# Softmax denominators in a cross-attention kernel: computed in four column quarters ahead of the weighted sums, with a half-width reciprocal copied to all rows

## The chip, the cores and the metric

The kernel runs on one core of one Trainium2 chip. The core has a matrix engine (PE, whose weight loads are listed apart as PEld), a vector engine (DVE), an activation engine (ACT), a general engine (POOL) and a queue engine (SP) that issues transfers. Each engine works through its own instructions in the order in which they were issued, and waits on semaphores for the others. Matrix products land in PSUM; everything else lies in SBUF. The metric is the device time of one execution in microseconds (us); lower is better.

## The reference

The layer is cross-attention followed by a feed-forward network, in float32, on 2048 query rows of width 256 and 1601 context rows of width 192, with 16 heads of width 64 and one learned null key and value ahead of the context. What matters here, per head:

```python
x = layer_norm(x, g_norm)
q = x @ Wq
kv = context @ Wkv
k, v = jnp.split(kv, 2, axis=-1)
...
sim = jnp.einsum('bhid,bhjd->bhij', q, k)
sim = jnp.where(full_mask[:, None, None, :], sim, max_neg)
attn = jax.nn.softmax(sim.astype(jnp.float32), axis=-1)
out = jnp.einsum('bhij,bhjd->bhid', attn, v)
out = out.transpose(0, 2, 1, 3).reshape(b, -1, INNER)
out = out @ Wout
```

The softmax is a sum of exponentials over 1602 keys for each head and query, and the output of each head is divided by that sum. After it come a layer norm, a residual, three dense layers with weights of plus and minus one and rectifiers between them, and another residual.

## The kernel before

**Units.** The attention goes over units `(p, b)`: a pair `p` of heads (8 of them) and a block `b` of 512 queries (4 of them), 32 units, numbered 0 to 31 in this document as `u` is in the code. The keys lie on the partitions in 13 tiles of 128 (the last has 66). The order of the instructions is the order of the program text (`tc.manual_schedule()`), on every engine.

**One unit.** For each key tile `k`, `exps` multiplies keys and queries on PE (L393, both heads side by side in the two halves of the array's rows, into the PSUM tile `sT`), and ACT takes the exponential (L406) into an SBUF tile `e`. Between them PE forms the maxima of the next unit: `max_chunk` (L356) writes a PSUM tile of the pool `flex`, and DVE reduces it (L359). The pool `flex` has two buffers, so a new tile there waits until the tile before the last one has been read. POOL adds the 13 tiles `e` up into `acc` (L621 the first, L623 the others); it finishes them well into the next unit. Then `weighted` multiplies the values with the tiles `e` into the PSUM tile `av` (L413): 13 key tiles, two heads each, the heads in the two halves of the array's columns. A float32 matmul goes through the array in two passes, so it has two records in the trace.

**The denominators.** `acc` of the unit before (`last`) holds partial sums on 128 partitions. `divided` (L428 to L435) completes them: two matmuls with a matrix of ones, one for each head (L431), write the sum of each of the 512 queries to 64 rows each, so that the PSUM tile `den` has every sum in all the 64 rows of its head. DVE takes the reciprocal of all 128 by 512 numbers (L433) and multiplies the unnormalised output `avs` of that unit with it (L434), in the SBUF tile `aoT`. It is called at L650, behind the third of the 13 key tiles of `weighted`.

**Behind it.** ACT copies `av` into `avs` (L671; one buffer, so it waits until L434 of this unit has read the old one). PE turns the maxima (L369), multiplies `aoT` with the output weights (`project_out`, L421), and projects queries, keys and values for the units to come (L213, L238, L243, L298, L310). DVE adds the result to `y_sb` (L424 in the first head pair, L426 later).

**Units that do more.** In units 0 and 1 the input rows of units 2 and 3 are normalised: DVE statistics, then on ACT a square root, eight instructions in `centred_beside` (L143, L144) and a table load for the exponential (L644). Units 30 and 31 normalise finished rows in the same way (L635 is the table load of unit 30). All of this is issued ahead of `weighted`. In unit 31 there is no next unit, so no maxima; POOL first multiplies and adds the finished rows of block 0 (L599, L600), then sums the exponentials. In units 28 and 29 DVE also turns the first feed-forward weights into numbers (L655, L657).

**The feed-forward.** The denominators of unit 31 come behind the first group of the second dense layer (L779, tile `den_last`); behind them DVE normalises rows of block 1, POOL adds their residual (L122, L123), DVE normalises again (L89), and PE turns the result (L130) behind the third group. In the feed-forward each dense group is 16 or 32 matmuls at L720, and `halved` (L708 on ACT, L709 on DVE) splits its result in two parts.

Of the kernel before, what the change touches and what calls it, by code (L numbers as in the profile page):

```python
# [9 lines left out]
F32 = mybir.dt.float32  # L10
# [12 lines left out]
HEADS, DH = 16, 64  # L23
# [13 lines left out]
def xattn_ffn(ctx, tc, x, ctxT, mask, g_norm, null_kv, wq, wkv, wout, g_out, k0, k1, k2, s0, s1, s2, out):  # L37
    nc = tc.nc
# [8 lines left out]
    def flex(name):  # L47
        return ps_f.tile([128, 2, 512], F32, tag="f", name=name)

    def spare(name):  # L50
        return ps_s.tile([128, 2, 512], F32, tag="s", name=name)
# [14 lines left out]
    lp = ctx.enter_context(tc.tile_pool(name="later", bufs=2))  # L66
    ones = cp.tile([128, DH], F32, name="ones")
# [27 lines left out]
    def slot(name):  # L95
        nonlocal n_slots
        n_slots += 1
        return (flex, spare)[n_slots % 2](name)

    def norm_begin(b, src, name):  # L100

        mv = stats(src[:, ts(b, 4), :], 4, f"{name}{b}")
        r = sp.tile([128, 4], F32, tag="rstd", name=f"rstd_{name}{b}")
        norms[b] = (mv, r)

    def norm_root(b):
        mv, r = norms[b]
        nc.scalar.activation(r, mv[:, :, 1], AF.Sqrt, bias=eps_sb)

    def norm_end(b, dst, src, beside=False):  # L110
        mv, r = norms[b]
        nc.vector.reciprocal(r, r)
        if beside:
            centred_beside(dst, src, mv, r, b)
            return
        for j in range(4 * b, 4 * b + 4):
            centred(dst[:, j, :], src[:, j, :], mv, r, j - 4 * b)

    def residual(b, engine):

        for j in range(4 * b, 4 * b + 4):
            engine.tensor_tensor(y_sb[:, j, :], y_sb[:, j, :], gout_sb, ALU.mult)  # L122
            engine.tensor_tensor(x_sb[:, j, :], x_sb[:, j, :], y_sb[:, j, :], ALU.add)  # L123

    def turned(b):

        pt = slot(f"uT_{b}")
        for j in range(4):
            for c in range(2):
                nc.tensor.transpose(pt[:, c, ts(j, 128)], y_sb[:, 4 * b + j, ts(c, 128)], ident)  # L130
        hi = lp.tile([128, 2, 512], F32R, tag="uhi", name=f"uhi_{b}", bufs=1)
        lo = lp.tile([128, 2, 512], F32R, tag="ulo", name=f"ulo_{b}", bufs=1)
        nc.scalar.copy(hi, pt)
        nc.vector.tensor_tensor(lo, pt, hi.bitcast(F32), ALU.subtract)
        return hi, lo
# [10 lines left out]
    with ExitStack() as att:  # L146
# [262 lines left out]
        def weighted(p, k, e, av):  # L409
            v = pairs[p][1]  # L410
            n = rows_of(k)
            for j in range(2):
                nc.tensor.matmul(  # L413
                    av[ts(j, DH), 0, :], v[:n, k, ts(j, DH)], e[:n, j, :], start=k == 0, stop=k == KC - 1
                )

        def project_out(p, b, aoT):
            po = spare(f"po_{p}_{b}")
            pv = po.rearrange("p a (c d) -> p (a c) d", d=D)
            for t in range(4):  # L420
                nc.tensor.matmul(pv[:, t, :], aoT[:, ts(t, 128)], weights[p][3], start=True, stop=True)  # L421
            y = y_sb[:, ts(b, 4), :]
            if p == 0:
                nc.vector.tensor_copy(y, pv)  # L424
            else:
                nc.vector.tensor_tensor(y, pv, y, ALU.add)  # L426

        def divided(p, b, avs, acc, ps):  # L428

            for j in range(2):  # L430
                nc.tensor.matmul(ps[ts(j, DH), :], ones, acc[:, j, :], start=True, stop=True)  # L431
            aoT = lp.tile([128, 512], F32, tag="aoT", name=f"aoT_{p}_{b}", bufs=1)
            nc.vector.reciprocal(aoT, ps)  # L433
            nc.vector.tensor_tensor(aoT, avs, aoT, ALU.mult)  # L434
            return aoT  # L435

# [142 lines left out]
        last = None  # L579
        with tc.manual_schedule():  # L580
            for u, (p, b) in enumerate(units):
# [21 lines left out]
                acc = lp.tile([128, 2, 512], F32, tag="acc", name=f"acc_{p}_{b}")  # L603
# [40 lines left out]
                    nc.scalar.activation(warm, eps_sb, AF.Exp)  # L644

                av = spare(f"av_{p}_{b}")
                for k in range(KC):
                    weighted(p, k, es[k], av)
                    if k == 2 and last is not None:
                        aoT = divided(*last, flex(f"den_{p}_{b}")[:, 0, :])  # L650
                if u in (len(units) - 4, len(units) - 3):

                    half = k0_u8[:, 2 * (len(units) - 3 - u) :, :][:, 0:2, :]
# [16 lines left out]
                avs = lp.tile([128, 512], F32, tag="avs", name=f"avs_{p}_{b}", bufs=1)  # L670
# [17 lines left out]
                last = (p, b, avs, acc)  # L688
# [11 lines left out]
    def second_weights(engine, c):  # L700
        if engine is nc.scalar:
            nc.scalar.activation(w1[c], k1_u8[:, c, :], AF.Identity, bias=s1b[:, 1:2], scale=s1b[:, 0:1])
        else:
            engine.tensor_scalar(w1[c], k1_u8[:, c, :], s1b[:, 0:1], s1b[:, 1:2], ALU.mult, ALU.add)
# [6 lines left out]
    def layer_open(b, n):  # L711
        return [fp.tile([128, 8, 512], F32R, tag=f"h{n}{part}", name=f"h{n}{part}_{b}") for part in ("hi", "lo")]

    def layer_pair(b, n, g, out, w, parts, chunks):

        ps = slot(f"ps{n}_{b}_{g}")
        steps = [(c, part) for c in range(chunks) for part in range(2)]
        for i, (c, part) in enumerate(steps):
            for f in range(2):
                nc.tensor.matmul(  # L720
                    ps[:, f, :],
                    w(c)[:, ts(2 * g + f, 128)],
                    parts[part][:, c, :],
                    start=i == 0,
                    stop=i == len(steps) - 1,
                )
        halved(out[0][:, ds(2 * g, 2), :], out[1][:, ds(2 * g, 2), :], ps)

    def first(b, uT):
        h0 = layer_open(b, 0)  # L730
        for g in range(4):
            layer_pair(b, 0, g, h0, lambda c: w0[:, c, :], uT, 2)
            if b == 0 and g < 2:
                second_weights(nc.scalar, 2 + g)
        return h0
# [31 lines left out]
    with tc.manual_schedule():  # L767
        for c in range(2):
            second_weights(nc.scalar, c)
        for c in range(4, 8):  # L770
            second_weights(nc.gpsimd, c)
        nc.gpsimd.tensor_scalar(w2, k2_u8, 2.0, -1.0, ALU.mult, ALU.add)
        h0 = first(0, uT)
        for b in range(NB):
            h1 = layer_open(b, 1)
            for g in range(4):
                layer_pair(b, 1, g, h1, lambda c: w1[c], h0, 8)
                if b == 0 and g == 0:
                    aoT = divided(*last, slot("den_last")[:, 0, :])  # L779
                if b == 0 and g == 1:  # L780
                    project_out(*last[:2], aoT)
                if b + 1 < NB:
                    if g == 0:
                        norm_begin(b + 1, y_sb, "y")
                        norm_root(b + 1)
                        norm_end(b + 1, y_sb, y_sb)
                        residual(b + 1, nc.gpsimd)
                    if g == 1:
                        norm_begin(b + 1, x_sb, "r")
                        norm_root(b + 1)  # L790
                        norm_end(b + 1, y_sb, x_sb)
                    if g == 2:
                        uT = turned(b + 1)
            if b + 1 < NB:
                h0 = first(b + 1, uT)
            third(b, h1)
# [39 lines left out]
```

## Time and profile before

| | |
|---|---|
| time, median of 3 runs (lowest, highest) | 1310.03 us (1309.79, 1311.21) |
| the profiled execution | 1309.9 us, of which span 1308.1 us |
| PE busy | 1290.2 us (99%) |
| POOL busy | 997.9 us (76%) |
| DVE busy | 819.7 us (63%) |
| ACT busy | 624.7 us (48%) |
| denominators on PE (L431), share of the chain | 2% |
| reciprocal on DVE (L433), 31 of them | 104.0 us, 3356 ns each |
| mean granted TensorE clock | 0.996 |

The span is the time from the first instruction to the last; the execution has 1.8 us around it. The page of the profile lists busy time by engine, a chain of waits followed back from the last instruction, and groups of instructions by line. Groups have the busy time of the group, the mean duration of one, and the idle time of the engine before them with what ended it. A busy PE is not one at its peak, since matmuls are pipelined and their ends are modelled. Paces are read from starts here, not from durations of matmuls.

### The profile page before, as it was taken

To read this page: it belongs to the slowest core of one execution; us is meant where nothing else is said; L and a number is where in the kernel's file an instruction comes from. 1 tells how busy PE (TensorE), PEld (TensorE's weight loads), DVE (VectorE), ACT (ScalarE), POOL (GpSimd) and SP (SyncE) were. 2 spreads that over 40 slices of the span, in tenths; PEclk is the share of its full clock that TensorE was granted. 3 is DMA by queue.
4 is the path that set the end of the run, shared out by engine and by line. 5 is a ranking of instruction groups with operands and counts; after the bars stand their busy time and mean duration, and the time that the engine had idled before them with its cause. 6 is when DMAs were issued, how large, how long until landed. Compare 5 with 4: busy or idle time off the path is not lost.

```text
span 1308.1 us, 15963 instructions
## 1 busy us (share of the span) xinstructions
PE 1290.2 (99%) x6568; PEld 657.8 (50%) x6568; DVE 819.7 (63%) x822; ACT 624.7 (48%) x740; POOL 997.9 (76%) x503
## 2 busy tenths in 40 slices
PE   8989999999999999999999999999999999999998
PEld 6334444444444444444444444444444443688887
DVE  7877666666666666666666666666666784554431
ACT  4576444444444444454555555555555457321121
POOL 4768988898889888998889888988898999611100
PEclk9989999999999999999999999999999999999999
DMA  6100000000000000000000000000000010000000
GB/s 143 21 1 5 1 1 13 6 1 1 13 5 1 1 13 5 1 1 5 9 5 1 1 13 5 1 1 5 1 17 1 1 41 1 1 9 9 17 17 17
DMA packets 16122, 13.18 MB, mean 10 GB/s; under 512 B 2656, under 2 KB 15520, under 8 KB 16048
## 3 DMA queue, kind: packets, MB, share of 16 engines
q1 hardware_dynamic: 14928, 11.02, 3.2%
q8 instruction: 52, 0.85, 0.3%
q10 hardware_dynamic: 640, 0.79, 0.2%
q0 software_dynamic: 480, 0.34, 0.2%
q14 instruction: 22, 0.18, 0.0%
HBM read 10.04 MB, written 2.10 MB: 9 GB/s over the span
## 4 chain that ended last, share of the span: by engine, by line
PE 91%; DVE 3%; ACT 2%; POOL 2%; DMA 1%; issue 1%; SPq 0%; DVEq 0%; POOLq 0%; ACTq 0%
PE sT L393 28%; PE av L413 26%; PE ps L720 9%; PE max L356 7%; PE psq L213 4%; PE po L421 4%; PE ps L746 2%; PE den L431 2%; PE psv L298 2%; PE psk L238 2%; PE sT L404 1%; DVE mx L359 1%; POOL acc L623 1%; PE psv L310 1%; DMA x_sb<-in_x 1%; PE psk L243 1%
## 5 line engine op out<-in xcount | busy, mean ns | idle before, releaser
L623 POOL TENSOR_TENSOR acc<-acc,e 128x1024 f32<-128x1024 f32 (+1 forms) x352 | 847.0, 2406 | 27.6
L359 DVE TENSOR_REDUCE mx<-max 128x2 f32<-128x1024 f32 x384 | 452.0, 1221 | 81.4 <-PE max L356 81.3
L406 ACT ACTIVATE e<-sT,maskb 128x1024 f32<-128x1024 f32 (+1 forms) x416 | 459.6, 1113 | 42.0 <-PE sT L404 11.8
L393 PE MATMUL sT<-qT,kT 64*128 64x512 f32 (+1 forms) x1664 | 448.5, 612 | 0.8 <-ACT e L406 0.2
L413 PE MATMUL av<-e,v 128*64 128x512 f32 (+1 forms) x1664 | 369.5, 594 | 0.2 <-ACT e L406 0.2
L356 PE MATMUL max<-kr,qr 64*128 64x512 f32 x768 | 292.4, 750 | 0.0
L413 PEld LDWEIGHTS av<-e,v 128*64 128x64 f32 (+1 forms) x1664 | 116.7, 137 | 237.7 <-issue 222.6
L393 PEld LDWEIGHTS sT<-qT,kT 64*128 64x128 f32 (+1 forms) x1664 | 130.4, 181 | 153.6 <-ACT e L406 144.3
L671 ACT COPY avs<-av 128x512 f32<-128x512 f32 x32 | 18.7, 585 | 321.6 <-PE av L413 321.6
L433 DVE RECIPROCAL aoT<-den 128x512 f32<-128x512 f32 x31 | 104.0, 3356 | 60.0 <-PE den L431 60.0
L621 POOL TENSOR_TENSOR acc<-e,e 128x1024 f32<-128x1024 f32 x32 | 75.6, 2362 | 70.1 <-ACT seen L611 58.4
L356 PEld LDWEIGHTS max<-kr,qr 64*128 64x128 f32 x768 | 76.1, 187 | 90.4 <-DVE mx L359 68.4
L371 DVE TENSOR_TENSOR mT<-mt,pick 128x512 fp32r<-128x512 f32 x32 | 22.1, 691 | 119.0 <-PE mt L369 119.0
L720 PE MATMUL ps<-h0hi,w 128*128 128x512 f32 x256 | 79.6, 392 | 0.1
L720 PE MATMUL ps<-h0lo,w 128*128 128x512 f32 x256 | 78.9, 389 | 0.0
L122 POOL TENSOR_TENSOR y_sb<-y_sb,gout_sb 128x256 f32<-128x256 f32 x12 | 9.3, 776 | 88.8 <-DVE y_sb L89 88.8
L214 ACT ACTIVATE qr<-psq 128x512 fp32r<-128x512 f32 x32 | 19.1, 597 | 100.0 <-PE psq L213 97.1
L213 PE MATMUL psq<-xnT,wq 128*128 128x512 f32 x124 | 60.2, 609 | 2.5 <-DVE xnT L463 2.5
L709 DVE SCALAR_TENSOR_TENSOR h1lo<-ps,h1hi 128x1024 fp32r<-128x1024 f32 x16 | 19.6, 1224 | 68.3 <-ACT h1hi L708 68.2
L708 ACT ACTIVATE h1hi<-ps 128x1024 fp32r<-128x1024 f32 x16 | 16.4, 1025 | 95.0 <-PE ps L720 95.0
L421 PE MATMUL po<-wo,aoT 128*128 128x256 f32 x256 | 60.6, 379 | 0.0
L404 PE MATMUL sT<-mT,ones_r 64*128 64x512 f32 x128 | 52.3, 787 | 1.3 <-DVE mT L371 1.3
(157 smaller groups left out, 1060.9 us busy)
## 6 DMA issues: line engine op xcount, KB each, us to landing
out_x<-o SPq DMA_DIRECT2D x7, 256.0 KB, 2.1
x_sb<-in_x SPq DMA_DIRECT2D x3, 512.0 KB, 8.2
wa<-in_wkv SPq DMA_DIRECT2D x8, 128.0 KB, 2.7
wq<-in_wq SPq DMA_DIRECT2D x8, 128.0 KB, 2.2
wo<-in_wout SPq DMA_DIRECT2D x8, 128.0 KB, 2.0
xnT<-in_k SPq DMA_DIRECT2D x1, 1024.0 KB, 5.7
wb<-in_wkv SPq DMA_DIRECT2D x15, 64.0 KB, 2.4
ctx_a<-in_ctxT SPq DMA_DIRECT2D x2, 256.0 KB, 8.1
```

Source lines behind the costliest of these rows:

```text
L213: nc.tensor.matmul(ps[:, 0, :], weights[p][0][:, c, :], xnT[:, b, c, :], start=c == 0, stop=c == 1)
L356: nc.tensor.matmul(ps[:, j, :w], qr[rows, ts(t, 128)], kr[rows, ds(start, w)], start=True, stop=True)
L359: nc.vector.tensor_reduce(maxima[p, b][:, t, :, c], ps[:, :, :w], AX.X, ALU.max)
L393: nc.tensor.matmul(ps[:n, j, :], kT[rows, ds(128 * k, n)], qT[rows, :], start=k < 2, stop=k >= 2, skip_group_check=k >= 2,)
L404: nc.tensor.matmul(ps[:n, j, :], ones_r[rows, :n], mT[rows, :], start=False, stop=True)
L406: nc.scalar.activation(e[:n], ps[:n], AF.Exp, bias=maskb[:n, k : k + 1])
L413: nc.tensor.matmul(av[ts(j, DH), 0, :], v[:n, k, ts(j, DH)], e[:n, j, :], start=k == 0, stop=k == KC - 1)
L421: nc.tensor.matmul(pv[:, t, :], aoT[:, ts(t, 128)], weights[p][3], start=True, stop=True)
L433: nc.vector.reciprocal(aoT, ps)
L621: nc.gpsimd.tensor_tensor(acc, es[0], es[1], ALU.add)
L623: nc.gpsimd.tensor_tensor(acc[:m], acc[:m], es[k][:m], ALU.add)
L720: nc.tensor.matmul(ps[:, f, :], w(c)[:, ts(2 * g + f, 128)], parts[part][:, c, :], start=i == 0, stop=i == len(steps) - 1,)
```

## The change

The two matmuls of a denominator become four. Each takes one head `j` and one half `h` of the 512 queries (256 columns) and multiplies with 32 columns of ones, so that it uses a quarter of the array's columns and fills 32 rows of PSUM: rows 64j + 32h onward hold head j, query half h. The four fill 128 rows by 256 columns. DVE's reciprocal then covers 256 columns and writes a new SBUF tile `r`. Eight copies on ACT, each 32 rows by 256 columns, spread `r` into `aoT`: each quarter to both 32-row halves of its head, in the columns of its query half. DVE's multiplication is as before, and waits for the copies.

The call moves, too: the four matmuls now stand ahead of the 13 key tiles of `weighted`, where they stood behind the third. The reciprocal, the copies and the multiplication are issued there as well. In the feed-forward the place is the same as before.

```diff
-        def divided(p, b, avs, acc, ps):
+        def denominators(acc, ps):
+
+            for h in range(2):
+                for j in range(2):
+                    nc.tensor.matmul(
+                        ps[ds(64 * j + 32 * h, 32), :],
+                        ones[:, :32],
+                        acc[:, j, ts(h, 256)],
+                        start=True,
+                        stop=True,
+                        tile_position=(0, 64 * j + 32 * h),
+                    )
+
+        def divided(p, b, avs, ps):
+
+            r = lp.tile([128, 256], F32, tag="r", name=f"r_{p}_{b}", bufs=1)
+            nc.vector.reciprocal(r, ps)
+            aoT = lp.tile([128, 512], F32, tag="aoT", name=f"aoT_{p}_{b}", bufs=1)
 
             for j in range(2):
-                nc.tensor.matmul(ps[ts(j, DH), :], ones, acc[:, j, :], start=True, stop=True)
-            aoT = lp.tile([128, 512], F32, tag="aoT", name=f"aoT_{p}_{b}", bufs=1)
-            nc.vector.reciprocal(aoT, ps)
+                for h in range(2):
+                    for rows in range(2):
+                        nc.scalar.copy(aoT[ds(64 * j + 32 * rows, 32), ts(h, 256)], r[ds(64 * j + 32 * h, 32), :])
             nc.vector.tensor_tensor(aoT, avs, aoT, ALU.mult)
             return aoT
...
                 av = spare(f"av_{p}_{b}")
+                if last is not None:
+                    den = flex(f"den_{p}_{b}")[:, 0, :256]
+                    denominators(last[3], den)
+                    aoT = divided(*last[:3], den)
                 for k in range(KC):
                     weighted(p, k, es[k], av)
-                    if k == 2 and last is not None:
-                        aoT = divided(*last, flex(f"den_{p}_{b}")[:, 0, :])
...
                 if b == 0 and g == 0:
-                    aoT = divided(*last, slot("den_last")[:, 0, :])
+                    den = slot("den_last")[:, 0, :256]
+                    denominators(last[3], den)
+                    aoT = divided(*last[:3], den)
```

## The prediction

> **What bounds the kernel now.** I read the page first: engines, then the chain.
>
> ```profile
> PE 1290.2 (99%) x6568; PEld 657.8 (50%) x6568; DVE 819.7 (63%) x822; ACT 624.7 (48%) x740; POOL 997.9 (76%) x503
> PE 91%; DVE 3%; ACT 2%; POOL 2%; DMA 1%; issue 1%; SPq 0%; DVEq 0%; POOLq 0%; ACTq 0%
> ```
>
> PE holds 91% of the chain, so a microsecond on PE counts, and one on DVE or ACT only where PE comes to wait for it. Next, the chain in order of time around one ordinary unit (9):
>
> ```profile
> 401.80 0.23 PE max L356 x2
> 402.03 2.73 PE av L413 x12
> 404.76 0.86 PE den L431 x4
> 405.62 8.59 PE av L413 x40
> ```
>
> The four denominator records take 0.86 us, as much as one key tile of `av` with its four. The two heads therefore run side by side, and each of the two passes takes 0.43 us. Then the timeline at the head of the weighted sums:
>
> ```profile
> 400.92 1.22 DVE L359 TENSOR_REDUCE mx<-max 128x2 f32<-128x1024 f32 x1
> 401.96 0.20 PEld L413 LDWEIGHTS av<-e,v 128*64 128x64 f32 x4 [0.56 <-ACT e L406]
> ```
>
> `av` starts at 401.96. The maxima tile before the last is read by DVE until 402.14. That tile's buffer is the one `den` gets, which today is of no interest, because `den` is issued two and a half microseconds later. Last, the stretches in which ACT has other work behind the exponentials, in unit 30:
>
> ```profile
> 1083.06 2.37 POOL L623 TENSOR_TENSOR acc<-acc,e 128x1024 f32<-128x1024 f32 x1
> 1083.85 2.12 DVE L434 TENSOR_TENSOR aoT<-avs,aoT 128x512 f32<-128x512 f32 x1
> 1085.77 0.20 ACT L635 ACTIVATE warm<-eps_sb 128x1 f32<-128x1 f32 x1
> 1087.75 1.89 PE L421 MATMUL po<-wo,aoT 128*128 128x256 f32 x8
> 1089.68 1.22 DVE L426 TENSOR_TENSOR y_sb<-po,y_sb 128x1024 f32<-128x1024 f32 x1 [1.04 <-PE po L421]
> ```
>
> The multiplication takes 0.69 us where POOL is idle (the 1141.94 row below). Here it lasts 2.12 and ends at 1085.97, 0.55 behind the end of POOL's sum (1085.43): it waits for the sum in flight. ACT is free only at 1085.97, and PE wants `aoT` at 1087.75.
>
> **The change, part by part.** The sum stands against the profiled execution, 1309.9 us (span 1308.1 and 1.8 around it); the median is 0.1 above it.
>
> *The four matmuls in an ordinary unit.* The removed part is 0.86 us. The new part streams half the columns, two passes of 0.215, so 0.43 if all four quarters run together, as the two halves do now. A change of the array's tiling is priced at the end of the feed-forward's first group:
>
> ```profile
> 1135.65 0.61 PE L720 MATMUL ps<-h0lo,w 128*128 128x512 f32 x2
> 1136.19 0.20 PEld L431 LDWEIGHTS den_last<-acc,ones 128*64 128x64 f32 x4 [0.35 <-issue]
> 1137.20 0.30 PEld L720 LDWEIGHTS ps<-h0hi,w 128*128 128x128 f32 x2 [0.81 <-issue]
> ```
>
> From 1136.19 to 1137.20 is 1.01 us, and 0.86 of it is streaming; the other 0.15 is some 0.05 of first weights and 0.1 of emptying (the second L720 record starts 0.23 after 1135.65 and streams 0.23, to 1136.11, and the next load begins at 1136.19). Today `den` and `av` share a tiling; with quarters one more change lies between them. What precedes is a change either way. The new wait: `den` starts when the reduction ends at 402.14, plus some 0.1 us for PE to see it, 402.24, which is 0.28 behind today's 401.96. All of `av` is queued behind it. So 0.28 + 0.03 (weights, 32 columns) + 0.43 + 0.09 (emptying) = 0.83 against 0.86: 0.03 us won. Over the 28 units 2 to 29, -0.8 us. Bounds for the parts that no row shows: if quarters and halves share a tiling, the 0.09 and the load of `av` (0.05) vanish, -0.14 more per unit; if only two quarters run at once, +0.43 per unit. I take the values in the sum, since the array's halves run fully together and every change of tiling in the trace has its gap.
>
> [...]
>
> *Reciprocal.* It lasts 3.36 us for 512 columns and 0.18 for 4 (L112), so 6.26 ns per column, and 1.75 for 256. DVE gains 1.6 us per unit, but in ordinary units DVE waits for PE afterwards (the turned maxima, L371, 119.0 us of waiting in 29 times), so this is worth nothing.
>
> *Eight copies.* ACT's plain copies last 585 ns for 512 columns and 175 for one; so 0.38 for 256. Two copies of 400 columns take 0.89 together at 0.50 each, so the second hides 0.1. Eight take 0.38 + 7 x 0.28 = 2.3 us. Upper bound: the 128x256 instructions of L143 read SBUF and last 497 ns, 4.0 for eight. In an ordinary unit ACT has nothing until `avs` 12 us after the start of `av` (its group has 321.6 us of idle time, 31 times). Reciprocal, copies, and a multiplication that may wait 2.4 for POOL end 9 us after that start: hidden, with 3 us to spare.
>
> *Where this cover is gone.* ACT works in order, and in units 1, 30 and 31 the copies are queued behind the normalisation and its table load.
>
> Unit 30: copies from 1085.98 to 1088.3; POOL's sums follow each other every 2.41 us, so without today's collision they end at 1085.43, 1087.84 and 1090.25; the multiplication ends at 1090.25 + 0.55 = 1090.8; `po` starts at 1090.95 (0.05 signal, 0.1 weights) instead of 1087.75: +3.2. Behind `po` PE holds unit 31. Any length of copies between 1.9 and 4.2 gives the same.
>
> Unit 1: ACT is free at 106.89, the copies end at 109.2, POOL's sums at 108.75 and 111.15 (today's multiplication, 104.77 to 106.89, ends 0.55 behind one at 106.34), the multiplication at 111.7; `po` at 111.85 instead of 109.56: +2.3.
>
> Unit 31: with the shift of 3.2 ACT is done with rows at 1117.3, copies at 1119.6, POOL's sum at 1120.7 (it starts 1.1 later, since L599 waits for L426, then at 1094.1 against 1093.03), multiplication 1121.25. `avs` has one buffer and waits for it: 1121.3 against 1117.53 + 3.2 = 1120.7, +0.6, and behind it on ACT are weights and the split that PE needs. Here no maxima hold `den` back: -0.3. Against that, today PE waits 0.3 us at 1128.45 for a split that POOL's last sum holds up; a later PE does not: -0.3.
>
> *The feed-forward.* The chain in order of time:
>
> ```profile
> 1138.56 3.36 DVE aoT L433
> 1141.94 0.69 DVE aoT L434
> 1142.63 0.35 DVE st_y L77
> ...
> 1153.84 1.41 PE uT L130 x8
> ```
>
> This chain goes on through DVE and POOL to 1153.84, where PE already waits 0.25 us. The reciprocal gives 1.6, the copies take 2.3 with 0.1 of signals: +0.8, all of it seen by PE. The 0.4 that PE wins in `den_last` only lengthens its wait.
>
> Sum: -0.8 + 2.3 + 3.2 + 0.6 - 0.3 - 0.3 + 0.8 = +5.5; 1309.9 + 5.5 + 0.1 = **1315.5 us**.
>
> **The rivals.** (a) No gap between quarters and halves: 28 x 0.14 = 4 us less, 1311.5. For: both stack 128 rows; against: each change shown in the trace costs. (b) Only two quarters at once: 28 x 0.43 = 12 more, 1327.5. For: no row has quarters; against: four records of two heads run in pairs without loss. (c) The other side, faster: the quarters stream while the last maxima leave the array, so that neither the wait nor the gaps show and `den` costs 0.43 alone. That is -0.43 x 28 = -12.0 in place of -0.8: 1304.3. It turns the sign once the gain passes 6.3 / 28 = 0.23 us per unit. Against it: the reduction ends at 402.14, after 401.96. (d) Dearer copies, over 4.2 us: each late multiplication misses one more sum of POOL, 2.4 in units 1, 30 and 31 each, and some 1.9 in the feed-forward: 1324. (e) The late units stay covered, because the copies get ahead of the normalisation: only -0.8 and the feed-forward's 0.8 remain, 1310. Against: in the order of instructions on ACT the copies stand behind the table loads.
>
> **How the numbers follow.** Main case 0.60 (1313 to 1319 by itself), (a) 0.13, (b) 0.10, (c) 0.05, (d) 0.07, (e) 0.05. The measurement of this kernel tells apart about 0.2%, 2.6 us. Slower by more (over 1312.6): main nearly all, (b), (d), a little of (a): 0.79. Same: most of (a), (e), a corner of the main case: 0.15. Faster: (c), a little of (e): 0.06. The range holds the main case, (a) and (d): 1310.5 to 1323.0; (b), (c) and (e) are left out, 0.20.
>
> **What would show it.** Right: `den` records of 128*32 in eights with starts in two steps 0.215 apart; the first `av` load about 0.83 behind today's place; in units 1 and 30 `po` waiting for DVE L434 by 2.3 and 3.2 us; the turn at L130 waiting 0.8 longer. Wrong: `den` spread over 0.86 or more (b); the first `av` load directly behind `den` (a); `den` starting before the reduction's end (c); copies of 0.5 us and more without overlap (d); units 1 and 30 as long as before (e).

## The result and the profile after

The changed kernel takes 1321.73 us (median of 4 runs, 1319.83 to 1322.68) against 1309.91 us of the kernel before in the same comparison. The ratio is 1.0087, 95% interval 1.0072 to 1.0102: slower by 11.8 us. The forecast had the sign and named the late units, but its +5.5 fell 6.3 us short. The profiled execution is the shortest of the four, 1319.83 us (span 1318.1), so the stages below add up to +9.9.

The page after, engines and the first line of the chain of waits (from the last instruction back, what each step waited for):

```profile
PE 1285.9 (98%) x6696; PEld 655.8 (50%) x6696; DVE 777.1 (59%) x822; ACT 730.1 (55%) x996; POOL 998.0 (76%) x503
PE 59%; POOL 25%; DVE 6%; ACT 5%; issue 3%; DMA 1%; POOLq 0%; SPq 0%; DVEq 0%; ACTq 0%
```

PE is busy 4.3 us less, and the kernel is longer: what PE lost, it lost waiting, or running slowly. POOL's 25% of the chain is new; it is to be distrusted, as the next fence shows.

The same marks in both traces give the account: the first `sT` record of a unit, the last sums of exponentials, the second turn of the feed-forward (L130), the end.

| mark | before | after | shift | so the stage ahead of it changed by | predicted |
|---|---|---|---|---|---|
| unit 1 starts | 80.64 | 79.72 | -0.91 | -0.91 (start-up) | 0 |
| unit 2 starts | 115.22 | 118.38 | +3.16 | **+4.07** (unit 1) | +2.3 |
| unit 30 starts | 1059.60 | 1063.64 | +4.05 | **+0.89** (28 units, 0.03 each) | -0.8 |
| unit 31 starts | 1089.57 | 1098.54 | +8.96 | **+4.91** (unit 30) | +3.2 |
| `den_last` | 1136.19 | 1144.36 | +8.16 | -0.80 (unit 31, first layer) | 0 |
| `uT`, second | 1153.84 | 1163.77 | +9.93 | **+1.77** (feed-forward chain) | +0.8 |
| end | 1308.12 | 1318.05 | +9.93 | 0 | 0 |

**An ordinary unit** (9), from the timeline of the changed kernel:

```profile
404.29 1.22 DVE L359 TENSOR_REDUCE mx<-max 128x2 f32<-128x1024 f32 x1
405.62 0.19 PEld L432 LDWEIGHTS den<-acc,ones 128*32 128x32 f32 x8 [0.85 <-POOL acc L640]
405.65 0.64 PE L432 MATMUL den<-acc,ones 128*32 128x256 f32 x8 [0.26 <-POOL acc L640]
406.22 0.20 PEld L413 LDWEIGHTS av<-e,v 128*64 128x64 f32 x4 [0.41 <-issue]
386.86 2.34 POOL L640 TENSOR_TENSOR acc<-acc,e 66x1024 f32<-66x1024 f32 x1
```

The eight records stand as forecast: the first weights of `den` come at 405.62, 0.11 behind the reduction's end (404.29 + 1.22 = 405.51), the sum of the exponentials takes 0.60 from weights to weights, and PE was idle 0.26 ahead of it. The releaser named is POOL, and that is a coincidence. `den` reads the sums of unit 8, whose last one (66 partitions, 386.86) had been done for 16 us; the sum that ends at 405.63 in the chain of waits belongs to unit 9. `den` has to wait for its buffer, which the reduction frees 0.12 before that sum ends. The trace separates the two: in all of units 1 to 30 the first weights of `den` come 0.115 to 0.116 behind the end of a reduction, while their distance from the nearest end of a POOL sum runs from -0.003 to 0.076. The 25% of the chain follow from this one wrong link in each unit: POOL has 24 to 27% in every kernel below with the sums at the new place, and 0 to 2% in e5, e6 and e8, which have them elsewhere.

**The late units**: unit 30, then unit 1, in the timeline of the changed kernel, and last the projection of unit 1 in the kernel before.

```profile
1089.93 3.29 ACT L450 COPY aoT<-r 32x256 f32<-32x256 f32 x8
1093.25 1.62 DVE L451 TENSOR_TENSOR aoT<-avs,aoT 128x512 f32<-128x512 f32 x1 [6.99 <-ACT aoT L450]
1094.93 3.68 PE L421 MATMUL po<-wo,aoT 128*128 128x256 f32 x8 [2.93 <-DVE aoT L451]
...
109.23 1.63 DVE L451 TENSOR_TENSOR aoT<-avs,aoT 128x512 f32<-128x512 f32 x1 [6.99 <-ACT aoT L450]
110.92 2.80 PE L421 MATMUL po<-wo,aoT 128*128 128x256 f32 x8 [2.06 <-DVE aoT L451]
```
```profile
109.56 1.89 PE L421 MATMUL po<-wo,aoT 128*128 128x256 f32 x8
```

Copies behind the normalisation, a multiplication that waits for POOL's sum in flight (1.62 and 1.63 where it takes 0.69 in the feed-forward; in both units it ends 0.55 behind the end of a sum, at 1094.87 and 110.86), a projection that waits: the predicted sequence, with the predicted waits. Against its unit's start `po` is 3.1 and 2.3 late. But the eight projection records take 3.68 and 2.80 us where they took 1.89. The stretches with the granted clock tell why. A row has the stretch and its length, the busy time and number of instructions on PE, PEld, DVE, ACT and POOL, then the granted clock (third from the end) and two figures on transfers; the last two rows are the same places in the kernel before:

```profile
111.97:115.36 3.39, 3.39 (x8) 2.00 (x7) 2.57 (x3) 0.28 (x1) 1.10 (x1) 0.50 0.00 0
1091.60:1094.90 3.30, 0.39 (x3) 0.14 (x1) 1.65 (x2) 1.58 (x4) 3.14 (x3) 1.00 0.00 0
1095.01:1098.40 3.39, 3.39 (x8) 2.38 (x8) 0.46 (x1) 0.72 (x2) 3.39 (x2) 0.50 0.00 0
1098.50:1101.00 2.50, 2.48 (x13) 0.99 (x12) 1.23 (x1) 1.00 (x1) 2.42 (x2) 1.00 0.00 0
```
```profile
111.97:115.36 3.39, 3.39 (x13) 1.58 (x13) 0.88 (x1) 1.08 (x2) 1.99 (x1) 1.00 0.13 39
1087.00:1091.00 4.00, 3.98 (x21) 2.04 (x17) 1.92 (x2) 0.67 (x2) 3.84 (x3) 1.00 0.00 0
```

After each wait the granted clock is 0.50 for 3.41 us by the trace's record of it (from 111.96 and from 1095.00). The projection's records show it: in unit 1 they start 0.216 apart up to 111.89 and 0.427 apart from 112.23 on, in unit 30 0.427 apart from the second on, and before 0.216 apart. At 0.50 a stretch of 3.41 us does, by estimate, the work of 1.7; so up to 1.7 us are lost while PE is busy throughout (3.39 of 3.39). Before, the same two places had a granted clock of 1.00.

**The feed-forward chain**:

```profile
1146.73 1.75 DVE L444 RECIPROCAL r<-den_last 128x256 f32<-128x256 f32 x1
1148.56 3.31 ACT L450 COPY aoT<-r 32x256 f32<-32x256 f32 x8 [3.01 <-DVE r L444]
```

The reciprocal is 1.61 shorter, as forecast. The copies take 3.31 and not 2.3: 0.40 each, and none begins before the last one ends.

### The profile page after: what moved, and what is told of

The parts are those of the page before. It is cut to its first block, busy times and chain, and to the rows that moved or that the text cites. A ratio compares the mean times of both kernels' runs of the same rounds, so it can differ in the third digit from the quotient of the medians.

```text
span 1318.1 us, 16454 instructions
## 1 busy us (share of the span) xinstructions
PE 1285.9 (98%) x6696; PEld 655.8 (50%) x6696; DVE 777.1 (59%) x822; ACT 730.1 (55%) x996; POOL 998.0 (76%) x503
## 4 chain that ended last, share of the span: by engine, by line
PE 59%; POOL 25%; DVE 6%; ACT 5%; issue 3%; DMA 1%; POOLq 0%; SPq 0%; DVEq 0%; ACTq 0%
PE av L413 25%; POOL acc L640 19%; PE ps L739 10%; PE po L421 4%; PE psq L213 4%; PE sT L393 4%; POOL acc L638 3%; DVE mx L359 3%; PE ps L765 2%; ACT e L406 2%; POOL kT L261 2%; PE psv L298 2%; PE psk L238 1%; PE den L432 1%; PE psv L310 1%
## 5 line engine op out<-in xcount | busy, mean ns | idle before, releaser
L413 PE MATMUL av<-e,v 128*64 128x512 f32 (+1 forms) x1664 | 364.2, 594 | 0.0
L450 ACT COPY aoT<-r 32x256 f32<-32x256 f32 x256 | 102.9, 402 | 66.9 <-DVE r L444 64.3
L451 DVE TENSOR_TENSOR aoT<-avs,aoT 128x512 f32<-128x512 f32 x32 | 47.4, 1481 | 117.2 <-ACT aoT L450 117.2
L421 PE MATMUL po<-wo,aoT 128*128 128x256 f32 x256 | 63.3, 392 | 5.3 <-DVE aoT L451 5.3
```

The costliest lines, as they stand in the source:

```text
L413: nc.tensor.matmul(av[ts(j, DH), 0, :], v[:n, k, ts(j, DH)], e[:n, j, :], start=k == 0, stop=k == KC - 1)
L450: nc.scalar.copy(aoT[ds(64 * j + 32 * rows, 32), ts(h, 256)], r[ds(64 * j + 32 * h, 32), :])
```

## The experiments

Theory A: the loss lies in the late stages (waits, half clock behind them, copies one after the other), and in the ordinary units the new place costs about what the quarters win. The rivals are named with each run. The table holds what each kernel's trace shows against the kernel before, by the marks above; the ratios are against runs of the kernel before beside them, with 95% intervals. Two stages are left out of it: the start-up, and the stretch from unit 31's start to `den_last`, which changes by -0.81 to +0.02 except in e7 (+8.20) and e9 (+1.25).

| kernel | us | ratio | unit 1 | one ordinary unit | unit 30 | feed-forward chain |
|---|---|---|---|---|---|---|
| the change | 1321.73 | 1.0087 [1.0072, 1.0102] | +4.07 | +0.03 | +4.91 | +1.77 |
| e1 | 1311.67 | 1.0013 [1.0003, 1.0022] | +0.34 | +0.03 | +0.32 | +0.01 |
| e2 | 1317.62 | 1.0063 [1.0048, 1.0078] | +2.83 | +0.03 | +3.24 | +1.76 |
| e3 | 1318.62 | 1.0067 [1.0050, 1.0083] | +0.32 | +0.31 | +0.32 | 0.00 |
| e5 | 1314.83 | 1.0040 [1.0025, 1.0055] | +4.07 | -0.14 | +3.24 | +1.77 |
| e6 | 1306.53 | 0.9973 [0.9963, 0.9982] | 0.00 | -0.14 | 0.00 | +0.03 |
| e7 | 1328.24 | 1.0143 [1.0126, 1.0159] | +5.60 | +0.03 | +1.42 | +1.78 |
| e8 | 1307.30 | 0.9981 [0.9972, 0.9991] | -0.01 | -0.09 | 0.00 | +0.03 |
| e9 | 1319.00 | 1.0072 [1.0057, 1.0087] | +2.83 | +0.03 | +5.04 | +0.12 |
| e10 | 1317.25 | one run | +2.37 | +0.03 | +3.23 | +1.75 |

### e1: the old form in the late stages

```
-                if last is not None:
+                if u in (1, len(units) - 2, len(units) - 1):
+                    aoT = halves_form(*last, flex(f"den_{p}_{b}")[:, 0, :])   # two matmuls, full-width reciprocal
+                elif last is not None:
...
+                    aoT = halves_form(*last, slot("den_last")[:, 0, :])
```

> Units 1, 30, 31 and the feed-forward's last sums keep two matmuls and a full-width reciprocal without copies, placed ahead of the weighted sums as in the changed kernel; the 28 units between them have quarters and copies. Theory A (the loss sits in the late units: PE waits 2.2 and 3.0 us for the multiplication behind the copies, and after each wait a stretch of 3.41 us at half clock costs 1.7 us more, and the feed-forward's chain is 1.76 longer): the costs of +4.07 in unit 1, +4.91 in unit 30 and +1.76 in the feed-forward go; what stays is 28 x 0.03 = 0.9 and some 0.3 of waiting for the reduction in each of units 1 and 30, less up to 0.9 that unit 0 won: 1310 to 1312 us. No stretch at half clock but the one near 70 us. Theory B (the quarters themselves cost in the ordinary units, and the late units only show it): at least 1317.

1311.67 us, and the losses are gone where they were: units 1 and 30 keep the 0.3 of the new place, and the granted clock is 1.00 around them (108 to 120 us and 1080 to 1100). Theory B falls: the 28 units between, with quarters and copies, cost 0.03 each as they did.

### e2: the waits filled with matmuls

```
+            for _ in range(filler):            # 9 in unit 1, 13 in unit 30
+                nc.tensor.matmul(ps[:, 1, :128], ident, ident, start=True, stop=True)
```

> The changed kernel, with 9 matmuls of 128x128 (0.215 us each) in unit 1 and 13 in unit 30 ahead of the output projection, into an unused bank: 1.94 and 2.80 us of work inside the two waits of PE; nothing else is changed. Theory A (the clock is halved for 3.41 us because PE stands idle for 2 to 3 us): the granted clock stays 1.00 in both units, the projection's records are 0.2155 apart again in place of 0.427, and the time falls by 2 x 1.7 = 3.4 us, to about 1318.3 against a median of 1321.7. Theory C (the slow records behind the wait come from something that the late multiplication brings, contention for its tile or the like, not from PE standing idle): records still 0.427 apart, time as the changed kernel's, 1321.7 +- 1.

The timeline of unit 30, then the stretch behind its wait with the granted clock:

```profile
1091.11 3.07 PE L371 MATMUL mt<-ident 128*128 128x128 f32 x26
1094.21 2.00 PE L423 MATMUL po<-wo,aoT 128*128 128x256 f32 x8
```
```profile
1094.50:1098.00 3.50, 3.47 (x16) 1.94 (x17) 1.63 (x2) 0.92 (x3) 3.50 (x2) 1.00 0.02 5
```

The multiplication is as late as in the changed kernel (it waits for the copies and takes 1.65), and PE does 44 useless records more (6740 against 6696), and the kernel is faster by 4.1 us in the median, by 1.24 + 1.67 = 2.9 in the two units of the trace. The projection is back to 2.00 us. So in these two places the slow records come from PE standing idle (unit 1 also has 1.00 behind its wait), not from what the late multiplication touches: theory C falls.

### e3: the new place alone

```
-                    den = flex(f"den_{p}_{b}")[:, 0, :256]
-                    denominators(last[3], den)
-                    aoT = divided(*last[:3], den)
+                    aoT = halves_form(*last, flex(f"den_{p}_{b}")[:, 0, :])   # still ahead of the weighted sums
```

> The old form everywhere (two matmuls of 64 rows by 512 columns, reciprocal of the full width, no copies), but issued ahead of the weighted sums, as in the changed kernel. Theory A (the place costs 0.28 us per unit, because the sums now wait for the reduction of the maxima; the quarters win 0.25 of it back): 30 units x 0.28 = +8.4, less up to 0.9 in unit 0: 1317 to 1318.5, with the sums' first weights 0.28 behind the old start of the weighted sums and the output projection nowhere late. Theory B (the place is free and the quarters cost): 1310.

```profile
404.88 1.22 DVE L359 TENSOR_REDUCE mx<-max 128x2 f32<-128x1024 f32 x1
406.20 0.23 PEld L444 LDWEIGHTS den<-acc,ones 128*64 128x64 f32 x4 [0.85 <-issue]
```

1318.62, a little above the range given: the place costs 0.31 per unit and not 0.28. The sums begin 0.1 behind the end of the reduction (406.10), and no projection is late. So the quarters give back 0.31 - 0.03 = 0.28 of it, and one part of the change pays for the other.

### e5: quarters at the old place

```
                 for k in range(KC):
                     weighted(p, k, es[k], av)
+                    if k == 2 and last is not None:
+                        den = flex(f"den_{p}_{b}")[:, 0, :256]
+                        denominators(last[3], den)
+                        aoT = divided(*last[:3], den)
```

> Quarters, half-width reciprocal and copies as in the changed kernel, but at the old place, after the third key tile of the weighted sums. Theory A (there is no wait for the reduction there; two changes of tiling instead of one more): each of the 28 ordinary units takes 0.43 + 2 x 0.1 + 0.06 = 0.69 where before has 0.86, -0.17 x 28 = -4.8 against before; the late units and the feed-forward cost what they cost in the changed kernel, +9.0 together: 1314. The copies end some 3 us later than in the changed kernel; if the multiplication then ends after the weighted sums in ordinary units, the projection waits there and the time is above 1322. Theory B (quarters cost as much at any place): 1319 to 1322.

1314.83. An ordinary unit gains 0.14 (0.17 expected), and the later copies are still hidden there. The late units came out unalike, +4.07 and +3.24. The stretches around the two waits, cut at steps of 3.4 us:

```profile
109.30:112.70 3.40, 1.16 (x6) 1.05 (x6) 1.63 (x1) 1.61 (x4) 3.32 (x2) 1.00 0.00 0
112.72:116.10 3.38, 3.38 (x7) 1.97 (x6) 2.57 (x3) 0.16 (x1) 0.99 (x1) 0.50 0.00 0
1085.50:1088.90 3.40, 2.16 (x11) 0.57 (x7) 0.00 (x0) 3.31 (x10) 3.32 (x2) 1.00 0.00 0
1088.90:1092.30 3.40, 1.53 (x7) 1.38 (x8) 2.23 (x2) 0.92 (x3) 3.32 (x2) 1.00 0.00 0
```

The steps are those of the trace's own half stretch, counted backwards and forwards from its start (112.71). In unit 1 the wait lies within one step (PE busy 1.16 of 3.40), and half clock follows. In unit 30 a longer wait (3.1 us) is shared by two steps, with 2.16 and 1.53 busy, and the clock stays at 1.00 (in the step behind them too). So in this trace one wait was followed by half clock, which costs up to 1.7 us, and a longer one was not; the two differ in how the steps divide them.

### e7: copies ahead of the normalisation

The block that issues `den`, reciprocal, copies and multiplication is moved up, from behind the normalisation of the unit to directly behind `max_combined`.

> The changed kernel with the sums, the reciprocal and the copies issued ahead of the normalisation of the same unit, so that ACT does the copies before the normalisation's square root and its table loads. Theory A (the late units lose because the copies stand behind the normalisation on ACT): the projection in units 1 and 30 is no longer late, +4.07 and +4.91 fall to under +0.6 each, no stretch at half clock there; the feed-forward's +1.8 and the ordinary units' +0.9 stay: 1312.5 to 1314. Rival D (the copies only pass the delay on: the normalisation, 3.3 us later on ACT, makes PE wait for its rows instead): one of units 1, 30 and 31 longer by 1.5 to 3.3 us at the turned rows, 1316 or more.

1328.24: theory A's remedy failed, and rival D was right, with more than it asked for: unit 31 alone is 8.20 longer. The timeline of unit 1:

```profile
103.06 1.51 DVE L451 TENSOR_TENSOR aoT<-avs,aoT 128x512 f32<-128x512 f32 x1 [3.37 <-ACT aoT L450]
104.50 0.41 DVE L77 BATCH_NORM_STATS2 st_x<-x_sb 128x6 f32<-128x256 f32 x1
110.40 0.44 PE L475 MATMUL xT<-ident,y_sb 128*128 128x128 f32 x2 [1.65 <-ACT y_sb L144]
```

What I had overlooked is the queue on DVE. The multiplication comes with the block, waits there 3.37 us for the copies and then for POOL, and the statistics of the normalisation (L77) are queued behind it. PE gets the normalised rows one tile at a time and waits ahead of each, in unit 1 and again in unit 31, whose turned rows (`uT`) come in four pieces from 1130.37 to 1134.82, where before they took 1.09 in one. The projection of unit 1 takes 3.28 again, and that of unit 31 3.29, where unit 1's took 1.89 before; the mean granted clock is 0.991, against 0.996 before. How much of the 8.20 is waiting and how much is clock was not separated.

### e9: the feed-forward's copies shared out

```
-                        nc.scalar.copy(aoT[...], r[...])
+                        copy = nc.vector.tensor_copy if split and h == 1 else nc.scalar.copy
+                        copy(aoT[...], r[...])             # split in the feed-forward's stage alone
```

> The changed kernel with the eight copies of the feed-forward's stage, and only those, shared out: four on ACT, four on DVE at the same time. Theory A (the feed-forward's chain is 1.76 longer because eight copies take 3.3 us one after the other on ACT, while the half-width reciprocal gives 1.6): four take 1.65, so the chain from the last sums to the turn ends 1.65 earlier and is at most 0.2 longer than before: about 1320.0 against 1321.7. Rival E (the chain is longer for something else, the order of DVE's or POOL's queue): the turn stays 1.5 or more late, 1321.7.

```profile
1151.54 1.19 DVE L451 COPY aoT<-r 32x256 f32<-32x256 f32 x4
1151.60 1.65 ACT L451 COPY aoT<-r 32x256 f32<-32x256 f32 x4 [3.01 <-DVE r L444]
```

The chain is 0.12 longer than before in place of 1.77: the length of the copies was all but 0.12 of it, and rival E falls. The whole is 1319.00, where 1320.0 was forecast; the four executions run from 1317.92 to 1321.36, and the traced one is the longest. In it the granted clock was 1.00 behind the wait of unit 1 (114.70 to 118.00; +2.83), and 0.50 behind that of unit 30 for two steps, from 1094.40 to 1097.70 and from 1097.80 to 1101.10 (+5.04), and so into unit 31 (+1.25).

### e6 and e8: versions that keep the gain

e6 has quarters at the old place in the 28 ordinary units and the old form elsewhere:

```
+                    if k == 2 and 1 < u < len(units) - 2:
+                        den = flex(f"den_{p}_{b}")[:, 0, :256]
+                        denominators(last[3], den)
+                        aoT = divided(*last[:3], den)
+                    elif k == 2 and last is not None:
+                        aoT = halves_form(*last, flex(f"den_{p}_{b}")[:, 0, :])
```

> Quarters and copies at the old place in the 28 ordinary units, the old form of two matmuls and a full-width reciprocal in units 1, 30 and 31 and in the feed-forward. Theory A (the quarters by themselves win 0.14 per unit there, and all losses come from the late stages and the new place): 1309.8 - 28 x 0.14 = 1305.9, faster than the kernel before. Theory B (some of the loss is in the ordinary units): 1309 to 1311.

e8 has the same late stages, but in ordinary units puts the quarters ahead of the last chunk of the maxima:

```
+                    if k == KC - 1 and 1 < u < len(units) - 2:
+                        den = flex(f"den_{p}_{b}")[:, 0, :256]
+                        denominators(last[3], den)
                     if nxt is not None:
                         max_chunk(*nxt, order[k])
```

> In the 28 ordinary units the quarters stand one step earlier than in the changed kernel, ahead of the last chunk of the maxima, so that their buffer is one whose reduction has long ended; the reciprocal stays behind the last reductions; units 1, 30, 31 and the feed-forward have the old form at the old place. Theory A (the wait for the reduction is what eats the gain in the new place): no wait of 0.28, but one more change of tiling: 0.43 + 2 x 0.1 + 0.06 = 0.69 in place of 0.86, or less if the last chunk had to wait for its own buffer anyway: -0.14 to -0.3 per unit, 1301.5 to 1306. Theory B (the quarters cost the same wherever they stand): +0.03 per unit, 1310.7.

The chain of waits around unit 9 in e6, then the timeline of the same place in e8:

```profile
404.76 0.57 PE den L432 x8
405.33 8.74 PE av L413 x40
```
```profile
400.49 2.37 POOL L652 TENSOR_TENSOR acc<-acc,e 128x1024 f32<-128x1024 f32 x1
402.33 0.64 PE L432 MATMUL den<-acc,ones 128*32 128x256 f32 x8
```

e6 takes 1306.53 us, 3.2 us (0.27%) less than the kernel before and 15 less than the change. The chain puts 0.57 in place of 0.86 for `den`; half of that gain goes to the two changes of tiling around it (8.74 against 8.59 in the piece behind). e8 gains 0.09 per unit and not 0.14 to 0.3: there is no wait for the reduction, but `sT` and the maxima, which overlapped before (sT's first weights to av's first weights: 1.24 us), are now apart (2.00 with `den` between). And e8 agrees on what releases `den`: here it starts in the middle of a POOL sum (400.49 to 402.86), so it does not need the sum in flight.

### e10: two buffers for the copy of the weighted sums

```
-                avs = lp.tile([128, 512], F32, tag="avs", name=f"avs_{p}_{b}", bufs=1)
+                avs = lp.tile([128, 512], F32, tag="avs", name=f"avs_{p}_{b}", bufs=2)
```
on top of e2.

> The kernel with the filled waits (9 and 13 matmuls of 0.215 us in units 1 and 30), and two buffers for the weighted sums' copy in place of one, so that ACT's copy need not wait for the late multiplication. With one buffer, unit 1 lost 2.83 us and unit 30 3.24 at full clock, where the prediction had 2.3 and 3.2. Theory F (the 0.5 us left over in unit 1 is that copy: behind it ACT has the split of the turned rows that the next queries need): unit 1 falls to 2.3, unit 30 stays at 3.2. Rival G (it is the projection itself, or DVE's queue behind the multiplication): unit 1 stays at 2.8.

The timeline of unit 1 in e10, then in e2:

```profile
110.08 0.58 ACT L692 COPY avs<-av 128x512 f32<-128x512 f32 x1
110.09 1.65 DVE L453 TENSOR_TENSOR aoT<-avs,aoT 128x512 f32<-128x512 f32 x1 [6.99 <-ACT aoT L452]
113.62 1.88 PE L213 MATMUL psq<-xnT,wq 128*128 128x512 f32 x4
```
```profile
109.83 1.63 DVE L453 TENSOR_TENSOR aoT<-avs,aoT 128x512 f32<-128x512 f32 x1 [6.99 <-ACT aoT L452]
111.55 0.58 ACT L692 COPY avs<-av 128x512 f32<-128x512 f32 x1 [1.75 <-PE mt L371]
113.69 1.98 PE L213 MATMUL psq<-xnT,wq 128*128 128x512 f32 x4 [0.18 <-DVE xnT L482]
```

Unit 1 falls from +2.83 to +2.37 and unit 30 stays: theory F. ACT's copy now goes beside the multiplication, not behind it, and the split of the turned rows behind it no longer holds up the queries (`psq`).

## Right and wrong, step by step

- **Four matmuls at once, and the gap of the tiling: right.** The quarters run together (0.60 from weights to weights, 0.55 predicted): the eight records of unit 9 start in two groups of four 0.215 apart, so they stream for 0.43, as the sum has it. Rivals (a), (b) and (c) are out: the gap behind the quarters is there, eight records of four quarters take 0.64 and not 0.86, and `den` starts behind the reduction. So is (d), since eight copies take 3.3 and not over 4.2, and (e), since units 1 and 30 are longer by 4.07 and 4.91.
- **The wait for the reduction: right in kind, a little too small.** 0.28 predicted, 0.31 in e3; what the quarters give back is 0.28 and not 0.31. Twice 0.03 with the same sign makes +0.03 out of -0.03; over 28 units that is 1.7 us of the miss.
- **Units 1 and 30: the step that failed.** The sum took the lateness of `po` (2.3 and 3.2; measured 2.3 and 3.1) for the cost of the unit. With PE kept busy in the waits it nearly is: +2.37 and +3.23 in e10, whose mean granted clock is 0.996, as before. What was left out is the half clock behind each wait: the sum gave it nothing, and it cost 1.24 and 1.67 us in the changed kernel's trace (by e2). In e5 it came behind one wait of two. The trace of before has a granted clock of 0.50 for 10.24 us from 69.13, where PE waits in unit 0 (the 8 in the third slice of the row below, from the page); the sum drew nothing from it.

```profile
PEclk9989999999999999999999999999999999999999
```

- **Unit 1, a smaller term.** The one buffer of `avs` was counted in unit 31 and forgotten in unit 1, where it costs 0.46 (e10).
- **Unit 31: 0 predicted, -0.80 measured.** The 0.6 for `avs` did not come: the multiplication began in the last 0.1 us of a POOL sum (1124.30, the sum ends at 1124.37), took 0.69, and the copy of `av` stood 0.11 behind the turn of the rows, as before. Unit 30's extra delay is not the reason, since e2, with unit 30 at the predicted +3.2, has the same 0.69 and -0.77. The parts of the -0.80 were not separated.
- **The feed-forward: mechanism right, copies mis-sized.** The overlap of 0.1 between two copies was taken from ACT copies of another shape; here each copy starts 0.01 to 0.04 behind the end of the one before. Eight of these take 3.31 and not 2.3; that is the 1.0 between +0.8 and +1.77. e9 shows that all but 0.12 of the stage's loss lies there.
- **The account.** 1.7 (ordinary) + 1.8 (unit 1) + 1.7 (unit 30) + 1.0 (feed-forward) - 0.8 (unit 31) - 0.9 (start-up) = 4.5 from rounded terms; 9.93 less 5.5 is 4.4. Open stays the distance of 1.9 between the profiled execution and the median. The record points at the clock: the mean granted clock is 0.993 in the profiled execution and 0.992 in the three longer ones, and one more step of 3.4 us at half clock would, by estimate, take 0.0013 off the mean and add up to 1.7 us. No trace of a longer execution of this kernel was taken, so this is not shown.
- **The range.** The main case ended at 1319 and did not hold the 1321.73. That the range did is luck: its upper end, 1323.0, was there for rival (d), which did not happen and whose own figure, 1324 (1324.6 by its terms), lies outside it.

## To carry to other kernels

A wait like the ones here (2.06 and 2.93 us of idle PE) is to be priced with what comes after it: look for half clock behind the waits that are already in the trace, and add half of such a stretch to the upper bound, here 1.7 us for each step of 3.4; it lasted two steps in e9 and three in unit 0 (10.24 us, before and after). A helper that is hidden in the ordinary unit must be costed in each unit where its engine has other work, and there the old form may simply be kept, as e6 does. A moved block stands in every queue that it uses: in e7 the copies came earlier on ACT, and the multiplication held up DVE.

## What the hardware showed unexpectedly

**The clock.** A wait of 2.06 us (unit 1) and one of 2.93 (unit 30) were each followed by 3.41 us at a granted clock of 0.50, but 3.1 us in e5 were not; there two steps of 3.4 us divide the wait, with 2.16 and 1.53 us of work left in them. The record of the clock in the changed kernel's trace is regular: from 67.59 us on it holds 0.50 for 10.24 us, 1.00 for 34.13, 0.50 for 3.41, 1.00 for 979.63, 0.50 for 3.41 and 1.00 for 218.45. Against 10.24 / 3 = 3.413 these are 3, 10, 1, 287, 1 and 64 steps. In the trace of the kernel before, the half stretch in unit 0 has the same 10.24.

PE's work in the step just ahead says much, but not all. Half clock followed 0.47 us of work (changed kernel, unit 30), 0.72 and 0.88 (unit 0, changed kernel and before), 1.34 (changed kernel, unit 1), 1.16 (e5, unit 1), 1.71 (e9, start-up) and 1.96 (e9, unit 30, 1090.90 to 1094.30); it did not follow 2.13 (changed kernel, start-up), nor the 2.16 and the 1.53 of e5. The 1.53 stands among those that half clock followed, so these figures give no limit, all the less as the ends of matmuls are modelled.

The start-up shows it too. Its work is the same (1.90 us of PE between 36.0 and 39.6 us in both traces below), but the steps cut it differently: the step around the wait near 38 us has 1.71 us of work in e9 and 2.13 in the changed kernel, and the step behind it has a granted clock of 0.50 in e9 alone (two rows of e9, then of the changed kernel):

```profile
36.24:39.65 3.41, 1.71 (x11) 0.81 (x9) 1.59 (x3) 0.93 (x3) 0.00 (x0) 1.00 0.19 43
39.65:43.06 3.41, 3.41 (x16) 1.87 (x16) 1.94 (x2) 2.01 (x2) 0.22 (x1) 0.50 0.00 0
```
```profile
36.87:40.28 3.41, 2.13 (x17) 1.37 (x18) 1.79 (x2) 1.12 (x2) 0.00 (x0) 1.00 0.01 2
40.28:43.69 3.41, 3.41 (x24) 1.70 (x22) 2.72 (x4) 3.22 (x3) 2.23 (x1) 1.00 0.00 0
```

Unit 1 starts 0.91 early in the changed kernel's trace and 1.18 late in that of e9, 2.1 us apart for the same code. In e3, e6, e8 and e9 unit 1 starts 1.15 to 1.38 late, in the other six changed kernels 0.91 early to 0.12 late.

**Copies within SBUF.** Eight copies of 32x256 on ACT take 3.3 us, 0.40 each, and four on DVE 1.19, so 0.30 each. On ACT it was not the length that surprised (0.38 had been estimated for 256 columns) but that none of the eight overlaps the next: in the feed-forward each starts 0.01 to 0.04 behind the end of the one before.
